# A state-space, attention, expert and feed block on one core: dense products spread evenly beside the attention, gates' rows by transfers, products of zeros in the attention's sums

## The chip, the cores and the metric

One core of a Trainium2 chip runs the whole program in one launch. The metric is the device time of one execution in microseconds (us), lower is better. Engines are called PE (matrix products), PEld (its weight loads), DVE (vector), ACT (activations), POOL, and SP (which only issues transfers here).

## What is computed

2048 tokens of 128 values go through two layers, four residual blocks in all, each on the layer-normed stream. Cut to what matters, with `ln` for a layer norm without weights:

```
x = x + ssd(ln(x))          # Mamba-2 like: projections, conv, 8 heads x 32, state 16, gate, projection
x = x + ffn0(ln(x))         # h = ln(x); a = h + causal attention (16 heads of 8, 2048 x 2048);
                            # a + sum over 8 experts of gate[e] * (gelu(ln(a) @ fc1[e].T + b) @ fc2[e].T + b2)
                            # gate: softmax over the best 2 of 8 logits, 0 for the others
x = x + scan(ln(x))         # Mamba-1 like: projection, conv, silu, 256 channels x 16 states:
                            # h[t] = exp(-n * delta[t]) * h[t-1] + delta[t] * B[n][t] * u[t]
x = x + feed(ln(x))         # gated product 128 -> 512, two products 512 -> 512 with gelu, 512 -> 128
```

All 8 experts are computed for every token, and the gates weigh their results.

## The kernel before, in words

**Tiling.** The tokens are cut into four chunks (c = 0 to 3) of 512. Activations lie with features on the 128 partitions and the 512 tokens of a chunk along the free dimension, so the common product is 128x128 weights with a moving 128x512 operand in f32. The profile records such an f32 product as two MATMULs ("x2" is one product).

**The attention** is cut into jobs (c, g), four heads to a job. `shift` (L287) finds each query's largest score: per step a pair of heads, L302 into the sums `ps_m`, and DVE's L312 takes the maximum. `weighted` (L327) computes the scores anew, keys on the partitions: per step two L352 (one per head of the pair, 32 rows each) and two L358 (they subtract the maximum, 32 rows), into the one buffer `ps_e`; ACT's exp (L362) reads it into `probs`; and per two steps L339 multiplies the probabilities with values and a column of ones, 9 columns a head, into `ps_o`. `in_step` lets `weighted` of a job and `shift` of the next go in step. There are 320 such steps of `weighted`, 32, 64, 96 and 128 for the four chunks; the key blocks on the diagonal are shorter.

**What stands beside it.** The other blocks are Python generators that yield a weight for the work they have just issued. `with_attention` (L200) takes them one after another, and after each yield of weight w it issues attention steps of weight w * RATE. So the distance between two yields of a block sets how many of its products stand together, and how many steps of the attention follow without one. `ssd(1)` to `ssd(3)` go beside the first jobs. Then comes `second_layers`: experts(0); scan(0) and experts(1) abreast; scan(1) and feed(0) abreast; experts(2); feed(1). RATE (L452) is the attention's weight over that of the work meant to lie beside it. What is left of the attention is then issued alone. After it, with more buffers, scan(2) goes together with experts(3), scan(3) with feed(2), and feed(3) alone; experts(3) needs the whole attention. A scheduler moves instructions within dependencies and priorities (the order of issue), so the order on each engine is near this, not equal to it; each engine runs its own queue in order.

**The experts** (L722). Per expert: two transfers bring fc1 and fc2 into `wide` (three buffers, SP's queue). The gates (tokens on partitions) are turned to rows by products with the identity, in two parts of f32r whose sum is exact (`ge2`, `ghi`, L773, `rows_in`); L719 then spreads the row of expert e over all 128 partitions by a product with a selecting matrix, and DVE copies it into `gb` (L785). Four products L789 with gelu on ACT (L790); yield 3.7; four products L794 into one sum `ps_c`; DVE's L796 adds the bias and multiplies by `gb`; POOL adds it up; yield 3.5.

**The scan** (L807). After projections, a convolution (L825, L827), softplus and `du`, each of the 16 states takes: SP's transfer of B's row, spread over the partitions (`bb`), ACT's exp (`da`, L863), DVE's product (L865) and two scans (L867), and a transfer from POOL's queue that adds `db` to a sum in memory (L876). `w_bd` holds B's rows twice (48 columns).

**The feed** (L896). Gate products L911 and L913; yield 7.0; two layers of 4 x 4 products L927, yielding 7.0 after each 8; then L937.

Of the kernel before, what the change touches and what calls it, by code (L numbers as in the profile page):

```python
# [19 lines left out]
P = 128  # L20
# [52 lines left out]
def two_layers(ctx: ExitStack, tc: tile.TileContext, a: dict, out: bass.AP):  # L73
# [125 lines left out]

    def with_attention(stages, rate):  # L200

        due = 0.0
        for w in stages:
            due += 1.0 if w is None else w * rate
            while due > 0:
                w = next(attending_all, 0.0)
                due = 0.0 if not w else due - w
# [41 lines left out]
    def prepare(c):  # L249
# [35 lines left out]
        yield 1.0  # L285

# [40 lines left out]
    def weighted(c, g):  # L327
# [16 lines left out]
        for kb in range(nk):  # L344
# [3 lines left out]
            for i in range(0, 4, 2):  # L348
# [20 lines left out]
                if i == 0 and waiting:  # L369
                    sum_up(*waiting.pop())  # L370
                yield 1.1
# [80 lines left out]
    RATE = (4 * 11.0 + sum(48.0 * (c + 1) for c in range(NC))) / (2.5 * SSD + 2 * (MOE + SCAN + FEED) + 0.6 * MOE)  # L452
# [239 lines left out]
    w_bd = load(wp, "w_bd", [P, 2, 3 * DS], "(k p) o -> p k o", p=P)  # L692
    w_u = load(wp, "w_u", [P, 2, DI], "(k p) o -> p k o", p=P)
    w_dt1 = load(wp, "w_dt1", [3 * DS, DI])
# [7 lines left out]

    zeros = side.line("zeros")
    nc.gpsimd.memset(zeros, 0.0)
    two_rows, minus_low, rows_in = {}, {}, {}
    scratch_b = [tc.dram_tile([DS, C], F32, name=f"scratch_b{i}") for i in range(2)]
    for n in (NE,):
        two_rows[n] = wp.tile([P, n], F32R, name=f"two_rows{n}")
        nc.vector.tensor_tensor(two_rows[n], ident[:, 0:n], ident[:, n : 2 * n], ALU.add)
        minus_low[n] = wp.tile([2 * n, 2 * n], F32R, name=f"minus_low{n}")  # L710
        nc.vector.tensor_scalar(minus_low[n], ident[0 : 2 * n, 0 : 2 * n], 0.0, None, ALU.mult)
        nc.vector.tensor_scalar(minus_low[n][:, n:], ident[0 : 2 * n, n : 2 * n], -1.0, None, ALU.mult)
        rows_in[n] = [wp.tile([P, C], F32R, name=f"rows_in{n}_{i}") for i in range(1)]
        for t in rows_in[n]:
            nc.vector.tensor_copy(t, zeros)

    def spread_row(pg, n, rows_of, i):

        nc.tensor.matmul(pg, two_rows[n][:, i : i + 1].to_broadcast([P, P]), rows_of, start=True, stop=True)  # L719


    def experts(c, z):  # L722
# [34 lines left out]
        ge2 = sp.tile([P, NB, 2, NE], F32, tag="ge2", name="ge2")  # L757
        for i in range(2):
            nc.vector.tensor_tensor(ge2[:, :, i], ge, top.unsqueeze(2).to_broadcast([P, NB, NE]), ALU.mult)
        pgt = z.bank([2 * NE, C])  # L760
        for b in range(NB):
            nc.tensor.matmul(
                pgt[:, b * P : (b + 1) * P],
# [315 lines left out]
```

## Time and profile before

| | |
|---|---|
| median of 7 runs | 1755.42 us (1746.52 to 1764.16) |
| the profiled execution | 1763.77 us; its span, first to last instruction, 1762.1 us |
| mean granted clock of PE | 0.822 |
| moved by transfers | 83.24 MB |

The stages, from windows of the trace (busy us of each engine; clock is the share of PE's full clock that was granted):

| us from the start | what runs | PE | DVE | ACT | clock |
|---|---|---|---|---|---|
| 0 to 151 | ssd(0), part of ssd(1) | 125.5 | 78.0 | 31.4 | 0.88 |
| 151 to 438 | ssd(1) to ssd(3), attention | 270.6 | 169.5 | 82.5 | 0.82 |
| 438 to 1440 | second layer, attention | 883.4 | 533.6 | 476.5 | 0.82 |
| 1440 to 1589 | scan(2), experts(3) | 102.4 | 104.2 | 74.9 | 0.82 |
| 1589 to 1762 | scan(3), feed(2), feed(3) | 110.9 | 88.6 | 60.5 | 0.77 |

How to read it: busy time of PE is counted from start to modelled end, so it grows when the clock is low. A row of a windows view holds from:to, its length, then for each engine busy us and, in brackets, the number of instructions, then the clock, the transfers' share of 16 engines, and GB/s. With a line or tile chosen, only those instructions are counted. The trace starts the attention's steps at 151 and ends them at 1440.

### The profile page before, as it was taken

What the parts mean: (1) busy time and instruction counts of PE and PEld (TensorE: products, weight loads), DVE (VectorE), ACT (ScalarE), POOL (GpSimd) and SP (SyncE); (2) the same over time, 40 slices, a digit from 0 to 9 for tenths busy, and PEclk for the clock granted to TensorE, in tenths of its full rate; (3) what the DMA queues carried; (4) which work ended last, traced back from release to release, by engine and by line L of the source; (5) the groups of instructions that cost most, each with busy time, mean ns of one, the idle gap of its engine ahead of it and who ended that gap; (6) DMA issues with size and microseconds to landing.
All of it is one profiled execution on the core that took longest, in us unless ns stands there. A gap on an engine that the chain in (4) does not pass through costs nothing. (4 is left out here: it accounts for less than half of the span.)

```text
span 1762.1 us, 16427 instructions
## 1 busy us (share of the span) xinstructions
PE 1492.9 (85%) x6306; PEld 648.6 (37%) x6306; DVE 974.0 (55%) x1556; ACT 725.8 (41%) x847; POOL 284.0 (16%) x316
## 2 busy tenths in 40 slices
PE   6898999999899988889987898788998888657628
PEld 3554445444333433233333332333333243223224
DVE  4555546556444574666567677585343026764950
ACT  2212222323444434545344454355653536543522
POOL 4321111211000010111111012020000001440220
PEclk9887888878798978879578977669996899768759
DMA  2000000000100100323220034330000122760850
GB/s 85 1 1 0 1 0 1 1 0 26 40 27 28 30 1 31 77 55 72 60 68 17 31 78 82 86 66 25 24 30 25 36 66 73 163 141 31 184 97 30
DMA packets 62494, 83.24 MB, mean 47 GB/s; under 512 B 4576, under 2 KB 28816, under 8 KB 62416
## 3 DMA queue, kind: packets, MB, share of 16 engines
q0 software_dynamic: 16320, 31.46, 10.3%
q1 hardware_dynamic: 45664, 49.68, 9.1%
q10 hardware_dynamic: 432, 1.06, 0.2%
q8 instruction: 49, 0.80, 0.2%
q14 instruction: 29, 0.24, 0.0%
HBM read 49.55 MB, written 1.18 MB: 29 GB/s over the span
## 5 line engine op out<-in xcount | busy, mean ns | idle before, releaser
L312 DVE TENSOR_REDUCE top<-ps_m 128x2 f32<-128x1024 f32 (+3 forms) x320 | 339.7, 1061 | 288.5 <-PE ps_m L302 166.5
L362 ACT ACTIVATE probs<-ps_e 128x1024 f32<-128x1024 f32 (+3 forms) x320 | 286.3, 895 | 513.3 <-PE ps_e L358 309.6
L302 PE MATMUL ps_m<-kR,qR 32*128 32x512 f32 (+3 forms) x640 | 191.3, 527 | 68.1 <-DVE top L312 57.0
L352 PE MATMUL ps_e<-qR,kR 32*128 32x512 f32 (+3 forms) x640 | 177.2, 525 | 27.9 <-ACT probs L362 27.3
L339 PE MATMUL ps_o<-probs,vv 128*9 128x512 f32 (+3 forms) x1152 | 172.2, 611 | 1.0 <-ACT probs L362 0.9
L302 PEld LDWEIGHTS ps_m<-kR,qR 32*128 32x128 f32 x640 | 79.5, 209 | 246.4 <-DVE top L312 138.1
L867 DVE TENSOR_TENSOR_SCAN db<-da,hlast,db 128x512 f32<-128x512 f32 x128 | 163.0, 1310 | 5.5 <-ACT da L863 3.5
L358 PE MATMUL ps_e<-sh,onesR 32*128 32x512 f32 (+3 forms) x640 | 149.7, 434 | 0.1
L352 PEld LDWEIGHTS ps_e<-qR,kR 32*128 32x128 f32 x640 | 70.4, 207 | 182.0 <-ACT probs L362 106.6
L789 PE MATMUL ps_a<-nT,wide 128*128 128x512 f32 x192 | 116.3, 714 | 6.5 <-ACT h L790 4.3
L794 PE MATMUL ps_c<-h,wide 128*128 128x512 f32 x192 | 103.9, 645 | 0.0
L798 POOL TENSOR_TENSOR acc<-acc,ye 128x512 f32<-128x512 f32 x28 | 43.6, 1557 | 329.2 <-DVE ye L796 329.2
L871 POOL COPY hlast<-db 128x2 f32<-128x2 f32 x48 | 29.3, 611 | 388.7 <-DVE db L867 388.7
L863 ACT ACTIVATE da<-dl 128x1024 f32<-128x1024 f32 x64 | 66.4, 1054 | 51.0 <-DMA db<-db 25.4
L865 DVE TENSOR_TENSOR db<-du,bb 128x1024 f32<-128x1024 f32 x64 | 78.0, 1228 | 15.9 <-issue 11.0
L790 ACT ACTIVATE h<-ps_a,cols 128x512 f32<-128x512 f32 x96 | 63.8, 686 | 55.8 <-PE ps_a L789 55.5
L358 PEld LDWEIGHTS ps_e<-sh,onesR 32*128 32x128 f32 x640 | 77.9, 221 | 3.0 <-issue 1.8
L927 PE MATMUL ps_a<-g,wide 128*128 128x512 f32 x96 | 59.2, 748 | 13.8 <-ACT g L930 13.8
L789 PEld LDWEIGHTS ps_a<-nT,wide 128*128 128x128 f32 x192 | 37.9, 220 | 47.1 <-issue 20.7
L362 ACT ACT_TABLE_LOAD x41 | 52.6, 1283 | 1.3 <-PE ps_e L358 0.6
L927 PE MATMUL ps_a<-h,wide 128*128 128x512 f32 x96 | 50.8, 662 | 1.0 <-ACT g L930 1.0
L375 DVE COPY os<-ps_o 128x512 f32<-128x512 f32 x16 | 10.9, 683 | 70.9 <-PE ps_o L339 70.8
(375 smaller groups left out, 2156.2 us busy)
## 6 DMA issues: line engine op xcount, KB each, us to landing
wide<-in_fc SPq DMA_DIRECT2D x64, 256.0 KB, 3.2
bb<-scratch_b SPq DMA_DIRECT2D x64, 256.0 KB, 3.4
db<-db POOLq DMA_DIRECT2D x32, 512.0 KB, 5.8
u<-db POOLq DMA_DIRECT2D x28, 512.0 KB, 5.8
wide<-in_h SPq DMA_DIRECT2D x16, 512.0 KB, 3.6
wide<-in_w SPq DMA_DIRECT2D x8, 256.0 KB, 2.9
x<-in_x SPq DMA_DIRECT2D x4, 256.0 KB, 5.4
w<-in_w SPq DMA_DIRECT2D x4, 256.0 KB, 3.9
```

What stands on the lines that cost most here:

```text
L302: nc.tensor.matmul(pss[:, j, 0:n], qR[hr, w - P : w], kR[hr, g, kc * C : kc * C + n], start=True, stop=not diag,)
L312: nc.vector.tensor_reduce(top[:, i : i + 2, kc], pss[:, :, 0:n], AX.X, ALU.max)
L339: pv = nc.tensor.matmul(o, v, prs[i // 2][:, i % 2, q0:], start=kb == 0, stop=kb == nk - 1)
L352: nc.tensor.matmul(pss[:, j, q0:], kR[hr, g, kb * P : (kb + 1) * P], qR[hr, q0:], start=True, stop=False)
L358: nc.tensor.matmul(pss[:, j, q0:], onesR[hr], sh[hr, q0:], start=False, stop=not diag)
L362: last = nc.scalar.activation(pr[:, :, q0:], pss[:, :, q0:], AF.Exp, scale=float(1.0 / np.sqrt(np.float32(HD))))
L789: nc.tensor.matmul(ph, we[:, 0, f * P : (f + 1) * P], nT, start=True, stop=True)
L794: nc.tensor.matmul(py, we[:, 1, f * P : (f + 1) * P], hs[f // 2][:, f % 2, :], start=f == 0, stop=f == NF - 1)
L863: in_turn("exp", nc.scalar.activation(da, dl, AF.Exp, scale=-float(n + 1)))
L865: nc.vector.tensor_tensor(db, du, bb.unsqueeze(1).to_broadcast(two), ALU.mult)
L867: nc.vector.tensor_tensor_scan(db[:, j, :], da[:, j, :], db[:, j, :], hlast[:, j, n : n + 1], ALU.mult, ALU.add)
L927: nc.tensor.matmul(ph, w[k // 2][:, k % 2, f * P : (f + 1) * P], h[k // 2][:, k % 2, :], start=k == 0, stop=k == NF - 1)
```

## The change

- **Spreading.** `experts` yields 0.9 after each of the first three products into `ps_c` and 0.8 after the fourth; `feed` yields 3.5 after each two of its gate products, and 0.9 or 0.8 after each single product of L927 (after's L916). `abreast` gets a share for each thread, by which its weights are passed on: 0.3 for a scan, 1.0 for experts and feed. RATE's divisor is 2.5 SSD + 3 MOE + 0.6 SCAN + 2 FEED in place of 2.5 SSD + 2 (MOE + SCAN + FEED) + 0.6 MOE, 401.1 in place of 440.7.
- **Gates by transfers.** The gates' rows are transposed in f32, copied to `gT`, written to memory (after's L762), and a transfer per expert brings row e to all partitions (after's L771). The products and copies with `rows_in`, `minus_low` and `two_rows` go.
- **Zeros.** `full` counts the weight of dense work issued, at most 1.0, less 0.7 per step of the attention. Where it is below 0, a step adds a product of the identity with 128x256 zeros to half of `ps_o` (after's L381), which changes no value, and counts 0.43 for it.
- `w_bd` and `w_dt1` lose the doubled 16 columns and rows.

```diff
+    full = [0.0]
     def with_attention(stages, rate):
         due = 0.0
         for w in stages:
+            full[0] = min(full[0] + (w or 0.0), 1.0)
             due += 1.0 if w is None else w * rate
...
+    zeros = ap.tile([P, 2 * P], F32, name="zeros")
+    nc.gpsimd.memset(zeros, 0.0)
...
                 if i == 0 and waiting:
                     sum_up(*waiting.pop())
+                full[0] -= 0.7
+                if full[0] < 0 and 0 < kb < nk - 1:
+                    nc.tensor.matmul(
+                        po[:, C - 256 :], ident, zeros[:, 0:256], start=False, stop=False, skip_group_check=True
+                    )
+                    full[0] += 256 * 4 / 2400
                 yield 1.1
...
-    RATE = (4 * 11.0 + sum(48.0 * (c + 1) for c in range(NC))) / (2.5 * SSD + 2 * (MOE + SCAN + FEED) + 0.6 * MOE)
+    RATE = (4 * 11.0 + sum(48.0 * (c + 1) for c in range(NC))) / (2.5 * SSD + 3 * MOE + 0.6 * SCAN + 2.0 * FEED)
...
-        pgt = z.bank([2 * NE, C])
...
-        gT = rows_in[NE][0]
-        ghi = z.line("ghi", (2 * NE, C), F32R)
-        nc.vector.tensor_copy(ghi, pgt)
-        nc.tensor.matmul(pgt, minus_low[NE], ghi, start=False, stop=True, skip_group_check=True)
-        nc.vector.tensor_copy(gT[0 : 2 * NE], pgt)
+        pgt = z.bank([NE, C])
+        for b in range(NB):
+            nc.tensor.transpose(pgt[:, b * P : (b + 1) * P], ge[:, b], ident)
+        gT = z.line("gT", (NE, C))
+        nc.vector.tensor_copy(gT, pgt)
+        gates = scratch_g[c % 2]
+        nc.sync.dma_start(gates, gT)
...
-            pg = z.bank([P, C])
-            spread_row(pg, NE, gT, e)
             gb = z.line("gb")
-            nc.vector.tensor_copy(gb, pg)
+            nc.sync.dma_start(gb, gates[e].partition_broadcast(P))
...
                 nc.tensor.matmul(py, we[:, 1, f * P : (f + 1) * P], hs[f // 2][:, f % 2, :], start=f == 0, stop=f == NF - 1)
+                if f < NF - 1:
+                    yield 0.9
...
-            yield 3.5
+            yield 0.8
...
-        yield 7.0
+            if f % 2:
+                yield 3.5
...
                         ph, w[k // 2][:, k % 2, f * P : (f + 1) * P], h[k // 2][:, k % 2, :], start=k == 0, stop=k == NF - 1
                     )
+                    if k < NF - 1:
+                        yield 0.9
                 in_turn("gelu", nc.scalar.activation(g[f // 2][:, f % 2, :], ph, AF.Gelu, scale=col(scale, f)))
-                if f % 2:
-                    yield 7.0
+                yield 0.8
...
                 if w is not None:
-                    t[2] += w
-                    yield w
+                    t[3] += w
+                    yield w * t[2]
...
-        yield from abreast((scan(0, scans), SCAN), (experts(1, side), MOE))
-        yield from abreast((scan(1, scans), SCAN), (feed(0, side), FEED))
+        yield from abreast((scan(0, scans), SCAN, 0.3), (experts(1, side), MOE, 1.0))
+        yield from abreast((scan(1, scans), SCAN, 0.3), (feed(0, side), FEED, 1.0))
```

## The prediction

> **What bounds the kernel now.** I read the engines' shares first, then the 40 slices, then the stages as windows, then single products.
>
> ```profile
> PE 1492.9 (85%) x6306; PEld 648.6 (37%) x6306; DVE 974.0 (55%) x1556; ACT 725.8 (41%) x847; POOL 284.0 (16%) x316
> PE   6898999999899988889987898788998888657628
> PEclk9887888878798978879578977669996899768759
> ```
>
> PE is the engine nearest to its limit, and in four fifths of the slices its busy digit is 8 or 9. But its granted clock (third line) is a 6, 7 or 8 in most slices, and twice a 5. A busy PE at 0.5 does half as much. So the question for this kernel is not only how much PE has to do, but at what clock. The stages between the start of the second layer and the end of the attention, in windows (PE, PEld, DVE, ACT, POOL busy, then the clock):
>
> ```profile
> 438.00:590.00 152.00, 142.98 (x610) 57.52 (x608) 70.46 (x107) 69.82 (x83) 7.61 (x6) 0.90 0.11 34
> 590.00:930.00 340.00, 294.43 (x1208) 111.86 (x1204) 205.39 (x291) 158.34 (x176) 44.35 (x49) 0.78 0.22 51
> 1064.00:1183.00 119.00, 94.79 (x442) 39.53 (x444) 80.91 (x94) 53.21 (x57) 21.33 (x23) 0.66 0.39 78
> 1183.00:1332.00 149.00, 142.13 (x709) 52.46 (x705) 71.06 (x88) 85.63 (x96) 8.93 (x8) 0.97 0.08 25
> 1332.00:1440.00 108.00, 96.35 (x383) 34.11 (x384) 12.29 (x31) 48.96 (x52) 3.79 (x4) 0.79 0.07 22
> ```
>
> They are experts(0); scan(0) with experts(1); the end of scan(1) with feed(0); experts(2); feed(1). Now the instructions of L352 alone, two for each step of the attention (one pair of heads, one key block), and then those that read `wide`, the expert and feed weights (two records to a product):
>
> ```profile
> 1064.00:1183.00 119.00, 23.14 (x66) 9.17 (x66) 0.66 0.39 78
> 1183.00:1332.00 149.00, 23.21 (x98) 9.07 (x96) 0.97 0.08 25
> ```
>
> ```profile
> 1064.00:1183.00 119.00, 11.71 (x18) 3.55 (x18) 0.66 0.39 78
> 1183.00:1332.00 149.00, 65.68 (x126) 21.16 (x126) 0.97 0.08 25
> ```
>
> This is the main reading. The first stage did 33 steps with 9 dense products in 119 us, 3.6 us a step; the second did 49 steps with 63 products in 149 us, 3.04 us a step. Nearly five times the dense work per step, and each step was shorter, because the clock was 0.97 instead of 0.66. (Scan(1), on DVE, is a second difference of the two; I come back to it.) That PE's busy share doesn't decide the clock is seen in two windows of 40 us:
>
> ```profile
> 840.00:880.00 40.00, 38.15 (x99) 13.76 (x100) 18.07 (x23) 15.50 (x18) 5.42 (x6) 0.53 0.27 53
> 1280.00:1320.00 40.00, 38.99 (x183) 13.65 (x181) 16.89 (x18) 23.28 (x25) 2.56 (x2) 1.00 0.08 27
> ```
>
> Both are busy over 95%, one at half the clock, one at full. The first holds 11 records on `wide`, the second 38. The attention's own products fill little of the array: L352, L358 and L302 have 32 rows of 128, and L339 mostly 9 columns of 128. What keeps the clock up seems to be products that use all rows and columns, arriving without long gaps. Here is an attention step at full clock with nothing dense beside it:
>
> ```profile
> 1380.77 1.03 ACT probs L362
> 1382.68 1.03 ACT probs L362
> 1384.59 1.02 ACT probs L362
> ```
>
> From exp to exp it is 1.91 us, of which ACT's exp takes 1.02 and L352 with L358 the rest; that is the floor of a step. One dense product of 128x512 (two records) takes 0.86 us more at full clock: in the chain of waits L927 x2 takes 1.06 us and x4 1.91.
>
> **The change, part by part.**
>
> *Spreading.* I counted, in the order of PE's instructions in both programs, the dense work after each of the 320 steps (f32 columns times four, f32r times two, in units of one 128x512 f32 product). Before, 51 steps stand in runs of three or more with less than half a product after each; after, 4. From step 64 to the end (the second layer's part) the real dense work goes from 358 to 377 units, since feed(1) now ends inside the attention and scan(2)'s first products (after's L808 to L871) stand before the last step. Half of feed(1)'s L927 did so already.
>
> *Zeros.* After's L381 stands 96 times in PE's order: 22 in the first 64 steps, 74 later. The trace of before has no 128x256 f32 product with these operands. The nearest row, 0.86 us for 512 columns, gives 0.43 at full clock and 0.86 at half; nothing, if it falls where PE waits for the exp. So 0 to 82 us; I take 0.43, 41 us in all, since most stand in front of the next L352 on PE's queue, and the step behind waits for them. Whether zeros as data hold the clock up no row can show: the gain of this part lies between none and the whole gain of even work. I take it that they count like other products, the rows of before telling instructions by shape and not by value.
>
> *The attention's part, summed.* After has 414 units in 256 steps (zeros counted as half a unit), 1.62 a step. The stage 1183 to 1332 is the template: by the program's order it had 1.34 units a step, took 3.04 us, at clock 0.97. The 0.28 units more cost 0.24 us, so 3.28 us a step, 840 us. To this I add two things. Scan(0) and scan(1) stand beside 113 of the steps, by the weights: RATE is now 524/401.1 = 1.31, a step of both parts weighs 1.5, so (62 + 0.3 x 46) x 1.31/1.5 = 66 and (40 + 13.8) x 1.31/1.5 = 47; DVE's work for one is 16 states of 1.23 + 2 x 1.31 = 3.85 us, 62 us, and L312's reductions share DVE in order with them. I charge a third of the 124 us, 41 us (0 to 124). ACT's order holds 160 table loads where it held 130, 28 of the 30 inside the attention, as exp and gelu now alternate oftener: 28 x 1.28 = 36 us of ACT, part of it beside PE's work; I charge 24. Sum 905 us, against 1002 now (438 to 1440): **-97 us**.
>
> *First layer's part* (151 to 438, 287 us at 0.82): 22 zeros cost 9 us, and its work isn't cut finer. I take the clock to give the 9 back: 0.
>
> *The gates.* Removed: 32 L719 and 32 L785 on the two rows below, plus L773. Added: four writes of 16 KB and 32 broadcasts of 256 KB on SP's queue. The nearest rows land in 1.6 us (`scratch_b`) and 3.4 us (`bb`).
>
> ```profile
> L785 DVE COPY gb<-ps_a x24: 664/680/692, 458.9 to 1323.0; 128x512 f32<-128x512 f32 x24
> L719 PE MATMUL ps_a<-rows_in,two_rows x24: 401/493/799, 458.1 to 1321.9; 128*128 128x512 f32 x24
> ```
>
> In SP's order the broadcast for expert e stands behind the weights that wait for expert e-2's buffer, so it goes out about one expert early; an expert takes 152/8 = 19 us in the first window, which covers 3.4. Of the copies' 22 us on DVE and L719's 20 us on PE I count nothing in the attention: the template stage had them, so what they cost there stays in the sum as a reserve of a few us. In the tail they were: PE sat idle 19.2 us before L789 for gb's copy. Against that eight broadcasts more, 2.1 MB, at the 160 to 200 GB/s moved there, take 10 to 13 us of queues on which the scans' accumulating transfers already end the chain. I let the two cancel.
>
> *The tail.* DVE was idle for 68 us before the attention's last copy, and scan(2)'s preparation came only then:
>
> ```profile
> 1436.72 0.69 DVE L375 COPY os<-ps_o 128x512 f32<-128x512 f32 x1 [68.30 <-PE ps_o L339]
> ...
> 1485.84 1.21 DVE L865 TENSOR_TENSOR db<-du,bb 128x1024 f32<-128x1024 f32 x1
> ```
>
> From the attention's end to the first state it takes 49 us. In after's order on DVE everything from layer norm to `du` and `u` (L802 to L843) stands ahead of that copy. What is late next is experts(3): its layer norm, gating and first expert, ahead of the first state on DVE; before, its first L796 came at 1474.7, 38 us after the copy, with PE shared. I take 31 us in its place: **-18 us** (-30 to 0). Bd's 16 columns fewer cost and give nothing, as 512 columns are streamed either way.
>
> **Sum.** 1763.8 (this execution's own time, 1762.1 of span) - 97 - 18 = 1649. The median of the runs shown is 1755.4, 8 us lower, so **1640**.
>
> A rule of the Trainium skill speaks against this: "TensorE: Matmul & The Clock Gate", section "What's actually happening", says that the monitor sets the clock by how busy PE has recently been, and throttles it after an idle window of about 3.4 us. By that, the window 840 to 880, 95% busy, would have had a full clock, and it had 0.53. Under the rule taken literally zeros and spreading would give no clock, and the sum would be the slower rival below. The trace decides against it here: it is the filling of the array that goes with the clock.
>
> **Rivals.**
>
> *No clock gained, zeros paid (slower).* If the clock follows something else, or products of zeros don't count and the even work isn't enough, the step keeps its present cost and the added work is paid. Before's own steps (from start to start of L352), sorted by the units that stand in three successive ones, took for the three 8.6 us (none), 8.5 (two), 10.7 (four), 12.9 (six); weighted with after's counts, they give 1022 us in place of 986 for the same 253 steps, +36; with the first layer's 9 and the tail's -18, 1791 here, **1782** by the median. It decides if the stages with 1.6 units a step show a clock under 0.85.
>
> *DVE and ACT become the bound.* In 590 to 930 DVE is busy 205 of 340 us, in order, with L312 and the scans; after gives these stages a quarter fewer steps (66 for 86, by RATE 1.19 without shares). If their steps don't shrink below 3.6 us, and the table loads (36 us) fall wholly on the path, the gain in the attention is 10 to 40 us: with the tail's 18 **1712**, by the median. For it speak the 57 us in which PE waits for DVE's L312; against it that no engine but PE is busy over 70% in any of these windows.
>
> *The scheduler undoes the spreading.* PE's order excludes it: 4 steps in long runs, not 51.
>
> *More than forecast.* With the template's step kept at 3.04 us, 778 us, the attention gains 224 and the whole ends near **1515** by the median.
>
> **Chances.** Forecast (1570 to 1700) 0.70; DVE and ACT (1700 to 1750) 0.14; no clock (1755 to 1800) 0.10; more than forecast (under 1570) 0.06. The range 1570 to 1740 leaves out 0.06 below and about 0.13 above. Faster by over 0.5% (9 us, about what a measurement of this kernel can tell from no change): 0.70 + 0.06 + 0.12 = 0.88; within it 0.03; slower 0.09.
>
> **What would show it.** Right: clock digits of 9 from the second layer on; the 256 steps (512 records) of L352's successor L360 in the second layer's part at 3.2 to 3.6 us each; the attention's last copy near 1340; first L853 within 31 us of it. Wrong: the same clock with 96 more products of L381; or a full clock with PE idle, behind ACT's table loads and L320's reductions. The first would overthrow the whole argument, the second only its size.

## The result and the profile after

The changed kernel took **1765.62 us** (median of 27 executions, 1746.75 to 1773.77), the kernel before 1752.55 on the same chips (67 executions): ratio **1.0083**, 95% interval 1.0066 to 1.0099. It is slower by 0.8%, clear of the noise, where the forecast was 1640 us. The profiled execution of after has a span of 1763.9 us and lies at its kernel's median; that of before (1763.8 us, clock 0.822) is one of its kernel's longer ones, so its stages are shown some us longer, and its clock lower, than is usual for it.

From the page of after: PE's line of the busy times, then PE's busy tenths and the granted clock in 40 slices.

```profile
PE 1497.6 (85%) x6446; PEld 656.1 (37%) x6446; DVE 953.4 (54%) x1512; ACT 765.5 (43%) x877; POOL 274.6 (16%) x316
...
PE   5898999999999898978988888999999887557638
...
PEclk9897796898989896986979867899999897768769
```

PE is as busy as before. The clock's row has five 9s in turn from the 27th slice on (1147 us and later), but from the 17th to the 26th (706 to 1147 us) it still goes between 6 and 9. So the clock is up in one place and not in another, and the stages show which. Windows of after (PE, PEld, DVE, ACT, POOL busy, clock): experts(0) and what leads to it; scan(0), scan(1) with experts(1) and feed(0); experts(2); feed(1).

```profile
428.00:686.00 258.00, 235.76 (x1029) 99.30 (x1028) 125.22 (x241) 102.51 (x120) 22.84 (x27) 0.85 0.12 34
686.00:1131.00 445.00, 382.63 (x1590) 147.56 (x1589) 299.62 (x375) 236.24 (x252) 72.48 (x83) 0.82 0.34 76
1131.00:1300.00 169.00, 157.53 (x768) 59.89 (x766) 71.06 (x89) 88.63 (x99) 10.18 (x9) 0.96 0.13 40
1300.00:1451.00 151.00, 135.33 (x647) 50.52 (x644) 44.29 (x65) 92.21 (x94) 3.81 (x4) 0.93 0.09 27
```

The same windows of after for L360 alone (two instructions to a step of the attention; PE, PEld, clock), for the scans' stage and that of experts(2):

```profile
686.00:1131.00 445.00, 56.20 (x200) 21.41 (x200) 0.82 0.34 76
1131.00:1300.00 169.00, 24.36 (x100) 9.53 (x100) 0.96 0.13 40
```

and for the dense products, those that read `wide` (two records to a product):

```profile
686.00:1131.00 445.00, 124.68 (x208) 39.83 (x206) 0.82 0.34 76
1131.00:1300.00 169.00, 67.15 (x128) 21.67 (x128) 0.96 0.13 40
```

In the scans' stage 100 steps and 104 dense products took 445 us, 4.45 us a step at clock 0.82; in experts(2)'s, 50 steps and 64 products took 169 us, 3.38 us a step at 0.96. The dense work per step is nearly alike now (1.04 and 1.28) and evenly spread in both. The first is not faster for it: before, the stage 590 to 1183 (290 instructions of L352, 145 steps, in 593 us) took 4.1 us a step. The two paces are not quite like with like: a step of this stage now has 0.4 units more beside it (1.6 for 1.2, 0.35 us at full clock), and 100 steps share the two scans where 145 did; the runs below are the firmer ground. The forecast's 3.28 us nearly held in the stage that it was read from, and not in the one that it was carried to. Nor did it hold in experts(0), which has no scan beside it either: from 479 to 648 us 41 steps and 64 products took 169 us, 4.1 us a step at clock 0.91. Steps 64 to 320 as a whole took 997 us before (438 to 1435) and 1023 after (428 to 1451), 74 products of zeros among them.

What one step of the scans' stage looks like is in the timeline of after (start, duration, engine, instruction, and in brackets the idle time before it and what ended it):

```profile
990.38 1.27 DVE L855 TENSOR_TENSOR_SCAN db<-da,hlast,db 128x512 f32<-128x512 f32 x1
...
991.63 1.27 DVE L855 TENSOR_TENSOR_SCAN db<-da,hlast,db 128x512 f32<-128x512 f32 x1
991.96 1.28 ACT L921 ACT_TABLE_LOAD   x1
...
992.21 0.28 PE L366 MATMUL ps_e<-sh,onesR 32*128 32x256 f32 x2
992.83 1.20 DVE L320 TENSOR_REDUCE top<-ps_m 128x2 f32<-128x1024 f32 x1
...
993.25 0.69 ACT L921 ACTIVATE g<-ps_a,cols 128x512 f32<-128x512 f32 x1
...
994.08 0.51 PE L310 MATMUL ps_m<-kR,qR 32*128 32x512 f32 x2 [1.59 <-DVE top L320]
...
994.71 2.02 PE L916 MATMUL ps_a<-h,wide 128*128 128x512 f32 x2
995.00 1.28 ACT L370 ACT_TABLE_LOAD   x1 [1.06 <-PE ps_e L368]
```

L310 needs `ps_m`, which L320 must have read; L320 stands on DVE behind the scan's two L855. So PE is idle for 1.59 us, and the dense product L916 that the change had put there can't use the gap: it stands behind L310 in PE's queue. On ACT a gelu (L921) brings two table loads, 1.28 us before it and 1.28 us before the next exp. And the L916 that follows runs at half the clock: 2.02 us for two records, where the one before this stretch, at 988.69, took 1.08.

### The profile page after: what moved, and what is told of

Read it like the earlier page. It is cut to its first block, busy times and chain, and to the rows that moved or that the text cites. A ratio compares the mean times of both kernels' runs of the same rounds, so it can differ in the third digit from the quotient of the medians.

```text
span 1763.9 us, 16756 instructions
## 1 busy us (share of the span) xinstructions
PE 1497.6 (85%) x6446; PEld 656.1 (37%) x6446; DVE 953.4 (54%) x1512; ACT 765.5 (43%) x877; POOL 274.6 (16%) x316
## 3 DMA queue, kind: packets, MB, share of 16 engines
HBM read 57.90 MB, written 1.25 MB: 34 GB/s over the span
## 4 chain that ended last, share of the span: by engine, by line
PE 60%; DVE 17%; ACT 8%; issue 7%; DMA 4%; POOL 3%; SPq 0%; POOLq 0%; ACTq 0%; DVEq 0%
PE ps_o L347 7%; PE ps_m L310 5%; PE ps_a L775 5%; PE ps_e L360 5%; DVE db L855 5%; PE ps_c L780 4%; DVE top L320 4%; PE ps_a L916 3%; PE ps_e L366 3%; PE ps_o L381 3%; ACT probs L370 3%; DMA db<-db 2%; DVE db L853 2%; PE ps_c L605 2%; PE ps_a L580 2%
## 5 line engine op out<-in xcount | busy, mean ns | idle before, releaser
L320 DVE TENSOR_REDUCE top<-ps_m 128x2 f32<-128x1024 f32 (+3 forms) x320 | 339.6, 1061 | 331.9 <-PE ps_m L310 187.8
L310 PE MATMUL ps_m<-kR,qR 32*128 32x512 f32 (+3 forms) x640 | 174.1, 508 | 50.9 <-DVE top L320 41.6
L360 PE MATMUL ps_e<-qR,kR 32*128 32x512 f32 (+3 forms) x640 | 165.4, 498 | 26.0 <-ACT probs L370 24.4
L855 DVE TENSOR_TENSOR_SCAN db<-da,hlast,db 128x512 f32<-128x512 f32 x128 | 165.1, 1331 | 15.1 <-ACT da L851 13.1
L347 PE MATMUL ps_o<-probs,vv 128*9 128x512 f32 (+3 forms) x1152 | 161.9, 568 | 1.5 <-ACT probs L370 1.5
L310 PEld LDWEIGHTS ps_m<-kR,qR 32*128 32x128 f32 x640 | 71.5, 202 | 195.6 <-DVE top L320 100.0
L366 PE MATMUL ps_e<-sh,onesR 32*128 32x512 f32 (+3 forms) x640 | 142.4, 414 | 0.8 <-DVE sh L332 0.8
L360 PEld LDWEIGHTS ps_e<-qR,kR 32*128 32x128 f32 x640 | 65.3, 195 | 172.2 <-ACT probs L370 94.6
L775 PE MATMUL ps_a<-nT,wide 128*128 128x512 f32 x192 | 110.5, 687 | 5.5 <-ACT h L776 5.4
L853 DVE TENSOR_TENSOR db<-du,bb 128x1024 f32<-128x1024 f32 x64 | 79.3, 1245 | 17.0 <-DMA db<-db 9.2
L916 PE MATMUL ps_a<-g,wide 128*128 128x512 f32 x96 | 66.4, 823 | 16.7 <-ACT g L921 13.5
L859 POOL COPY hlast<-db 128x2 f32<-128x2 f32 x48 | 20.5, 428 | 379.3 <-DVE db L855 373.8
L366 PEld LDWEIGHTS ps_e<-sh,onesR 32*128 32x128 f32 x640 | 71.8, 205 | 6.6 <-issue 5.4
L381 PE MATMUL ps_o<-zeros,ident 128*128 128x256 f32 x192 | 69.0, 443 | 0.0
L916 PE MATMUL ps_a<-h,wide 128*128 128x512 f32 x96 | 51.3, 660 | 6.1 <-ACT g L921 6.1
```

The costliest lines, as they stand in the source:

```text
L310: nc.tensor.matmul(pss[:, j, 0:n], qR[hr, w - P : w], kR[hr, g, kc * C : kc * C + n], start=True, stop=not diag,)
L320: nc.vector.tensor_reduce(top[:, i : i + 2, kc], pss[:, :, 0:n], AX.X, ALU.max)
L347: pv = nc.tensor.matmul(o, v, prs[i // 2][:, i % 2, q0:], start=kb == 0, stop=kb == nk - 1)
L360: nc.tensor.matmul(pss[:, j, q0:], kR[hr, g, kb * P : (kb + 1) * P], qR[hr, q0:], start=True, stop=False)
L366: nc.tensor.matmul(pss[:, j, q0:], onesR[hr], sh[hr, q0:], start=False, stop=not diag)
L381: nc.tensor.matmul(po[:, C - 256 :], ident, zeros[:, 0:256], start=False, stop=False, skip_group_check=True)
```

## The experiments

Each was timed beside the kernel before on the same chip, and the ratio is to that. Some runs leave instructions out or put another function in the place of gelu, so their results are not the block's; they are there for their times. "Gates alone" and such names are used below. Times are medians; the clock is the median over a kernel's executions; lines are those of after where nothing else is said.

### First: the three parts one by one

After the result three readings stood against one another, A, B and C of the expectations: the zeros cost more than they give back; the zeros carry the clock; the broadcasts crowd the tail.

**The change without its zeros**

```diff
-                full[0] -= 0.7
-                if full[0] < 0 and 0 < kb < nk - 1:
-                    nc.tensor.matmul(po[:, C - 256 :], ident, zeros[:, 0:256], ...)
-                    full[0] += 256 * 4 / 2400
```

> The changed kernel without the 96 products of zeros (results unchanged). Theory A, the zeros cost more than the clock they give: 96 x 0.43 = 41 us of PE go, the mean clock falls from 0.851 only a little (0.83 or more), and the time falls by 15 to 40 us, to 1725-1750, below before's 1752. Theory B, the zeros carry the clock and something else in the change costs: clock back to 0.82, time 1770 to 1800. In between (1755 to 1770): the zeros pay just for themselves.

1740.2 us, ratio 0.9932 (0.9904 to 0.9959). The zeros cost 25 us.

**The kernel before with zeros** (the counter `full` and L381 put in; the trace has 148 of the products, 296 records)

> The kernel before with the zeros alone, set by the same counter; as its dense work is less even, the counter puts 147 of them. Theory A: 147 x 0.43 = 63 us of PE are added, the clock rises to 0.86 or more, and the time is 0 to 40 us over before's, 1752 to 1792. Theory B: the clock's gain outweighs them, 1700 to 1745.

1769.6 us, 1.008 (1.0044 to 1.0115): +17 us (14 by the ratio) for 63 us of products (148 x 0.43), clock 0.860 for 0.829.

**The kernel before with the spreading alone** (RATE, shares, yields; 158 table loads for 130)

> The kernel before with the spreading alone (yields, shares, RATE), without zeros and with the gates as before. Theory A (steps outside experts(2) are held by DVE and ACT, not by the clock, and 28 more table loads and more work inside the attention are paid): 1755 to 1785. Theory B, my prediction's reading (even work raises the clock and so shortens steps): 1690 to 1735 at a clock of 0.86 or more.

1758.4 us, 1.0056 (1.0022 to 1.009): +6 us, where the forecast had its whole gain. The clock did rise (0.840 for 0.829), but span times clock rose too (from 1452 to 1477 us), by work or waits that are added; what the clock won went there.

**The kernel before with the gates alone** (transfers for L719 and L785, 16 columns fewer)

> The kernel before with the gates' rows by transfers alone (and the 16 columns fewer). Theory C, the 32 broadcasts crowd the transfers of the scans in the tail: slower than before by 5 to 20 us, 1757 to 1772, the tail after the attention longer than 327 us. Otherwise the removed copies and products show: 5 to 20 us faster, 1732 to 1747. The clock stays at 0.82.

1731.5 us, 0.9876 (0.9836 to 0.9917): **-21 us**, the only part that gains. The clock is 0.839 for 0.829, where it was expected to stay. Added to before, gates -21, then spreading (1740.2 - 1731.5) +9 and zeros +25 give +13, which is the change. On the gates alone the spreading gave no clock either (0.840 for 0.839).

### Second: why the spreading gave nothing

The expectations set two theories against one another. Filling theory, the forecast's: the clock follows how much of the array the products fill, so even products raise it. Stall theory: PE waits behind DVE's scans and ACT's tables, the clock falls in those waits, and products behind a blocked queue can't help.

**Without the scans** of the first two chunks (left out: 64 L867 of the kernel before)

```diff
-            for j in range(2):
+            for j in range(2 if c > 1 else 0):
                 nc.vector.tensor_tensor_scan(
```

> The kernel before, leaving out both scans L867 of each state for scan(0) and scan(1) (32 states, 64 instructions of 1.31 us, 84 us of DVE beside the attention); L865, the transfers and all products stay. Stall theory (the clock falls in windows in which PE waits for DVE's maxima or ACT's exps, because those engines are busy with other work, and not where the order has few dense products): the clock in the stages with the scans (0.77) rises to 0.85 or more with no product added, and the time falls by 50 to 110 us. Filling theory (my prediction's: the number of dense products per step sets the clock): the clock there stays near 0.77 and the time falls by under 40 us.

1699.0 us, 0.9699 (0.9631 to 0.9768), -53 us. The stage of the scans in windows of before, and of this run:

```profile
652.00:1195.00 543.00, 461.67 (x1995) 178.08 (x1993) 347.34 (x434) 254.17 (x277) 77.89 (x85) 0.78 0.26 59
```

```profile
644.00:1119.00 475.00, 423.90 (x1957) 166.59 (x1956) 271.23 (x366) 250.43 (x273) 75.65 (x85) 0.83 0.31 67
```

76 us less of DVE, and the stage is 68 us shorter at a clock of 0.83 for 0.78, with no product added (it also holds 132 steps for 136, some 15 us). DVE is busy 64% there, and yet of the 80 us of scans that are left out 53 are off the whole run. The stall theory's clock of 0.85 wasn't reached.

**The change with tanh for gelu** (the first three chunks of experts and first two of the feed; the feed's line is shown, that of the experts has `c > 2`)

```diff
-    in_turn("gelu", nc.scalar.activation(g[f // 2][:, f % 2, :], ph, AF.Gelu, ...))
+    in_turn("gelu", nc.scalar.activation(g[f // 2][:, f % 2, :], ph, AF.Gelu if c > 1 else AF.Tanh, ...))
```

> The changed kernel with tanh in place of gelu for the experts and feeds beside the attention (experts 0 to 2, feed 0 and 1), a function that needs no other table than exp: 74 table loads are left of 160, 110 us of ACT go; all else is the same. Stall theory: the exps come earlier, PE waits less, the time falls by 25 to 70 us and the clock rises by 0.01 or more. Filling theory: ACT was busy 43% and the loads lie beside PE's work; within 10 us of the changed kernel's 1765.

1691.6 us, 0.9664 (0.9607 to 0.9721): 74 us below the change. The gelus' own time stays (0.69 us each); what goes are 86 table loads. The group that names it, the loads ahead of the attention's exp, of after and then of this run:

```profile
L370 ACT ACT_TABLE_LOAD x52 | 66.7, 1283 | 4.3 <-PE ps_e L366 2.4 <-PE ps_e L368 1.1
```

```profile
L370 ACT ACT_TABLE_LOAD x12 | 15.4, 1283 | 0.3
```

86 x 1.28 = 110 us of ACT, an engine that is busy 43%, were worth 74 us, a little over the 25 to 70 expected.

**Spreading without the feed's yields** (on the kernel before; 134 loads)

> The kernel before with RATE, the shares and the experts' finer yields, but the feed's yields as before: 134 table loads, where the whole spreading had 158 and before has 130. If the feed's 24 more table loads are what spreading costs, the time is 5 to 25 us under that of the whole spreading (1758), 1733 to 1753. If not, it stays at 1755 to 1760.

1745.1 us, 0.9982 (0.995 to 1.0014). 13 us less than the whole spreading, which has 24 loads more: the feed's single products, each with a gelu between the attention's exps, cost more than they give.

**Zeros in every step that takes them** (on the kernel before; the trace has 256 of the products, 512 records)

```diff
+                if 0 < kb < nk - 1:
+                    nc.tensor.matmul(po[:, C - 256 :], ident, zeros[:, 0:256], ...)
```

> The kernel before with a product of zeros in every step in which one may stand: 252 of them, 108 us of PE at full clock. Stall theory: zeros cannot be issued while PE stalls, so the clock still falls about as often; they pay back about half their price (0.03 of clock per 63 us were seen), and the time rises by 20 to 60 us, to 1772-1812, at a clock of 0.87 to 0.90. Filling theory: every step is now over the threshold, the clock goes to 0.94 or more, and the time is at or under 1752.

1790.0 us, 1.0215 (1.0142 to 1.0287), clock 0.875. Zeros do raise the clock (0.832 for before), and pay back some 72 of their 109 us (256 products).

### Third: cheaper ways, on the gates alone

**Gates, pace, shares and experts' yields**

> The gates by transfers, the new pace and the threads' shares, and the experts' yields within the second product; the feed's yields as before and no zeros. If the parts add up, this is the run with the gates alone (1731.5 us) less what the spreading without the feed's yields gave on the kernel before (1745.1 against 1752.5, 7 us): 1724 us, 1716 to 1732, ratio near 0.984. Filling theory (even products raise the clock): the clock over the run rises by 0.02 or more against the gates alone and the time falls by 20 us or more, below 1712. Stall theory: the clock moves by less than 0.01, and what the table loads cost sets the rest.

1731.2 us, 0.9873 (0.9839 to 0.9907): nothing beyond the gates.

**Gates, and yields between the scan instructions**

```diff
             for j in range(2):
+                yield 0.6
                 nc.vector.tensor_tensor_scan(
...
-            yield 2.0
+            yield 0.8
```

> The gates by transfers, and beside them one edit in the scans: of the yield of 2.0 units behind each state, 0.6 is put ahead of each of its two scan instructions, so that the attention's maxima on VectorE can come between them and not only behind a whole state (about 3.9 us of VectorE); the sum of the yields is the same, and 8 table loads more come of it (138 for 130). Stall theory: TensorE waits less often behind VectorE, so the stage of the scans gets 10 to 25 us shorter, less 4 to 7 us for the loads: 1712 to 1728 us, clock up by 0.005 to 0.015. Filling theory: no product is added or spread, so the time stays at 1731 or rises by the loads, 1731 to 1740 us.

1730.8 us, 0.9858 (0.983 to 0.9886). The stall theory's 10 to 25 us didn't come. So it is not that two scans stand together; letting maxima between them moves the wait and doesn't remove it: in the profiles PE waits 56.8 us for the maxima (L310 for L320) with the gates alone, and 59.6 here.

**Gates, and the feed's products by four**

```diff
-                if f % 2:
-                    yield 7.0
+                if f == NF - 1:
+                    yield 14.0
```

> The gates by transfers, and beside them one edit in the feed: its yield comes behind four groups of products, not behind two, so that four gelus follow one another: 119 table loads for 130, and its sixteen products stand in one block of 14 us of TensorE. Stall theory with the price per load of the earlier runs (0.5 to 0.9 us): 6 to 10 us less than the gates alone, 1721 to 1726 us. Filling theory: the products are bunched more, the attention's steps between are emptier, so the clock falls and the time rises by 5 to 15 us, 1736 to 1747 us.

1758.4 us, 1.0011 (0.9988 to 1.0035): 27 us slower than the gates alone (24 by the ratios), with 11 loads fewer. Here the filling theory had the sign right, though its 5 to 15 us were too little, and the stall theory was wrong.

**The three together**

> The three together: gates, pace and shares and experts' yields, scan yields, feed by fours (124 table loads). Stall theory, by the sum of its terms: 7 us from the experts' spreading, 5 to 15 us from the scans, 6 to 10 us from the feed, so 1700 to 1715 us. Filling theory: the scans' edit gives nothing and the feed's costs, 1725 to 1740 us.

1738.7 us, 0.9905 (0.9871 to 0.9939). The time lies in the filling theory's range (1725 to 1740), and for its reason: by the single runs the scans' edit gives nothing, and it is the fours that cost. But beside the new shares they cost 7 us and not 27.

### Fourth: both theories apart, with the loads taken out

Fours cost 27 us, singles 13 (against pairs). The loads run the other way from the bunching, so they were taken out: tanh for gelu in all four kernels.

**Gates alone with tanh** (pairs, 65 loads)

> The gates by transfers, with tanh for gelu in the first three experts' and the first two feeds' chunks (so the function is another; its duration is the same, and it shares a table with the attention's exponentials): 65 table loads for 130. By the price of the earlier run (74 us for 86 loads): 56 us less than the gates alone, 1675 us, 1660 to 1690. It is the base of the two that follow.

1698.4 us, 0.9673 (0.9646 to 0.97). That is 33 us less than the gates alone (36 by the ratios), where 56 were expected: a load is worth less here than in the change.

**The change without zeros, with tanh** (singles, 74 loads)

> The change without its zeros, with tanh for gelu as in e13: spread singly, 74 loads. Loads theory (spreading fills the array, and the table loads that it adds took the gain back): with the loads out it is 30 us or more below e13, 1645 us or less, clock up by 0.02 or more. Stall theory (spreading gives next to nothing, since TensorE's queue stands behind VectorE): within 15 us of e13, 1660 to 1685 us. Against the run of the change with tanh (1691.6), zeros out: 20 to 30 us less, 1662 to 1672, if the zeros' price does not hang on the loads.

1665.6 us, 0.9483 (0.9454 to 0.9512): 33 us below the pairs, as the loads theory had it, with 0.016 more of clock (it had 0.02). The change with zeros and tanh took 1691.6, so the zeros cost 26 us here too: their price doesn't hang on the loads.

**Gates and fours with tanh** (62 loads)

> e13 with the feed's products by four (62 loads): if bunching itself cost the 27 us of the run by fours, it is 25 to 40 us above e13, 1700 to 1715 us; if it was another cause that hangs on gelu's tables, it is within 8 us of e13.

1731.1 us, 0.9855 (0.9824 to 0.9887): 33 us above the pairs, so bunching itself costs.

So with the loads out, the order that the forecast argued from is there: fours 1731, pairs 1698, singles 1666, 33 us for each step. Span times clock, which is PE's time at full clock, is 1424, 1423 and 1421 us, and the clock 0.824, 0.839 and 0.854: **the whole difference is clock.** From the first product of experts(0) to the attention's end, in windows of fours, pairs and singles:

```profile
443.00:1395.00 952.00, 836.47 (x3714) 319.27 (x3710) 504.73 (x676) 386.95 (x458) 106.53 (x110) 0.82 0.21 52
```

```profile
451.00:1367.00 916.00, 811.69 (x3697) 307.72 (x3697) 502.56 (x676) 384.86 (x457) 105.70 (x110) 0.85 0.22 53
```

```profile
467.00:1352.00 885.00, 783.29 (x3705) 299.49 (x3703) 508.82 (x687) 393.44 (x462) 101.23 (x111) 0.88 0.24 58
```

DVE's and ACT's busy times are alike within 3%; the clock differs (0.82, 0.85, 0.88), and PE's busy time with it. From fours to pairs only the feed's yields differ. From pairs to singles the pace and shares do too, and by the profiles 15 us lie ahead of the attention's end (1367, 1352) and 11 behind it, where scan(2)'s preparation is already done (the two executions profiled differ by 26 us, the medians by 33). So the gain is real, but a fraction of the forecast's, and with gelu's own tables the same edit costs 9 us.

**Singles with tanh and without the scans** (the 64 scan instructions left out as above)

> e14 without the scan instructions of the first two chunks (64 of them, 82 us of VectorE, left out; tanh for gelu as there). Stall theory: what holds the clock down are waits behind VectorE and ScalarE, so with both out it rises: 45 to 60 us less than e14 (53 us was the price on the kernel before), 1605 to 1625 us, the clock of the second part at 0.92 or above. If the forecast's figure holds at all (0.97 beside the attention), 1580 us or less. Filling theory alone: no product is added, so the time falls by VectorE's own share at most, and the clock stays within 0.01 of e14.

1611.3 us, 0.9172 (0.9144 to 0.92), 54 us less than with the scans.

```profile
463.00:1296.00 833.00, 754.73 (x3703) 290.99 (x3702) 434.94 (x623) 392.29 (x462) 97.69 (x111) 0.92 0.25 61
```

L360 has 496 instructions in this window, 248 steps, so a step takes 3.36 us at clock 0.92. Only here, with neither wait, the whole stretch goes at about the pace that the forecast gave it, 3.28 us (and that had zeros in it); the clock of 0.97 that it was to have isn't reached even so.

### Fifth: can the change keep its gelu?

**Singles, the gelus held back in pairs** (137 loads, no zeros, nothing left out)

```diff
-                in_turn("gelu", nc.scalar.activation(g[f // 2][:, f % 2, :], ph, AF.Gelu, ...))
+                held_ph.append((f, ph))
+                if f % 2:
+                    for i, p in held_ph:
+                        in_turn("gelu", nc.scalar.activation(g[i // 2][:, i % 2, :], p, AF.Gelu, ...))
+                    held_ph = []
```

> The change without its zeros, the feed's products spread singly as in the change, but its gelus held back and issued two together (the first of a pair waits in its PSUM bank for the second): 137 table loads for 160, nothing left out. Loads theory: 23 loads fewer at 0.5 to 0.9 us are 12 to 20 us off the 1740 of the run without zeros, so 1718 to 1730 us, and the clock rises by 0.005 to 0.01. If the loads are not what took the gain back: 1735 to 1745 us.

1733.7 us, 0.989 (0.9853 to 0.9928). 6 us under the change without zeros, by intervals that overlap, for 23 loads fewer (12 to 20 us were expected); no faster than the gates alone. Inconclusive: the held products also keep both buffers of `ps_a`, which the scan beside them needs, and no run takes that apart.

**The same, with the scans' products on POOL**

```diff
-            nc.vector.tensor_tensor(db, du, bb..., ALU.mult)
+            (nc.gpsimd if c < 2 else nc.vector).tensor_tensor(db, du, bb..., ALU.mult)
```

> e17, with the product ahead of each scan in the first two chunks on GpSimd for VectorE: 32 products of 128x1024, 40 us of VectorE. Stall theory: the price of VectorE's time in the runs without scans, 54 us for 82, gives 26 us less than e17, 15 to 30. Against it: GpSimd took 1.5 us for a product of half the size, so about 3 us stand in each state's own chain in place of 1.25; if that chain becomes the bound, or GpSimd slows VectorE, the time is that of e17 or up to 20 us above.

1740.3 us, 0.9937 (0.9906 to 0.9968). 40 us less work on DVE, and 7 us slower. The groups of the scan instructions (there L849; idle time before them and what ended it last) without and with the products on POOL:

```profile
L849 DVE TENSOR_TENSOR_SCAN db<-da,hlast,db 128x512 f32<-128x512 f32 x128 | 164.0, 1320 | 19.0 <-ACT da L845 17.3
```

```profile
L849 DVE TENSOR_TENSOR_SCAN db<-da,hlast,db 128x512 f32<-128x512 f32 x128 | 169.0, 1358 | 42.9 <-ACT da L845 21.1 <-POOL db L847 20.3
L847 POOL TENSOR_TENSOR db<-du,bb 128x1024 f32<-128x1024 f32 x32 | 78.1, 2444 | 90.9 <-DVE du L835 75.8 <-issue 15.1
```

POOL takes 2.44 us for what DVE does in 1.25, and DVE now stands idle 24 us more ahead of the scans, with the attention's maxima queued behind: PE waits 57.2 us for them (L310 for L320), where it was 48.3 in the run without POOL's products. The wait was moved, not removed.

## Why the prediction was wrong

| term | forecast, us | measured, us | by |
|---|---|---|---|
| spreading, beside the attention | -97, zeros' 32 in it: -129 | +9 | without zeros against gates alone |
| zeros | +32 there, +9 - 9 in the first layer | +25 | after against without zeros |
| gates | 0 | -21 | gates alone |
| tail | -18 | within the above; profiled -14 | last copy of `os` to the end, 325.4 and 311.0 |
| sum | -115 | +13 | |

**The step that failed** is the one called the main reading, with the sum built on it: that the stage 1183 to 1332 is "the template" for all 256 steps because its clock of 0.97 came from its even dense products, while scan(1) was only "a second difference of the two", charged with a third of DVE's time. The stage that was carried over has no scan beside it. In after it took 3.38 us a step, and the scans' stage, given the same evenness, 4.45. The runs price the waits that the template lacked, or that the spreading adds. The 64 scan instructions, 82 us of DVE, cost 54 us, where 41 were charged for all 124 us of the two scans (53 on the kernel before, so the price does not hang on the order). The loads cost far above the 24 that were charged: spreading (with the tail that goes with it) gives 33 us where loads are few (65 and 74) and takes 9 where they are not (130 and 160), so the loads took **42 us** back, all that it gave and more. Taking loads out gave 0.51 us for each with the gates alone (33 us for 65) and 0.87 with singles (75 us for 86). How much of the 42 is their number and how much their place, no run tells. The number added isn't all of it: with the gelus held back in pairs the spreading has 7 loads more than the gates alone and still gives nothing (1733.7 for 1731.5), unless the buffers that it holds are what costs.

Taken in a row, the runs come down from before's 1752 us to 1611: 21 us by the gates, 33 by leaving out 65 loads, 33 by the spreading, 54 by leaving out the scans. So what the forecast took for the price of uneven products (129 us) was in the main the price of other waits; evenness is worth 33 us, and that only where gelu's loads are out. What the row does not explain is experts(0) in after: without a scan, and with as many loads (16) as experts(2), it took 4.1 us a step for 1.9 units. By the pace of experts(2) (3.38 us for 1.55 units) and 0.86 us for each further unit it would be 3.7; the rest is open. The template was too low there too.

The mechanism of that step was half right. In the traces of before, of after and of the runs with tanh the clock is either full or half, and its changes lie whole multiples of 3.41 us apart. I cut the second layer's part into windows of 3.41 us on these changes, and worked out for each the filled share of the array (rows x columns x cycles of all products) and PE's busy share. Of two windows at full clock, one followed by a drop and one not, the first is the less filled in 98% of pairs, before and after. But PE's busy share orders them as well (99% and 98%), so the falls don't tell the two apart. What empties a window at full clock is mostly PE standing idle: each one with PE busy under 0.60 (16 before, 17 after) was followed by half the clock, and none with PE busy over 0.90. For the clock's return neither share decides so well (filling orders 89% of the pairs of windows at half before and 70% after, the busy share 89% and 84%). For filling speaks that nine windows in a row, 846 to 876 us of before, stayed at half with PE busy 0.87 to 1.00.

Drops come as often after the change as before (27 and 26). What the change shortens is the time until the clock comes back: 103 windows at half before, 80 after. The three orders with tanh show the same: by fours, by pairs and singly the clock falls 24, 25 and 22 times, and is at half for 99, 78 and 62 windows. Without the scans it falls 16 times for 22, and 40 windows for 62 are at half. So even products help a clock that is low; they don't stop it from falling while PE's queue is blocked. These counts are from one profile each.

The Trainium skill's rule that the prediction weighed and set aside ("TensorE: Matmul & The Clock Gate", section "What's actually happening": the monitor looks at how busy PE was, and throttles after an idle window) was the nearer one for the falls, though a window with PE idle for 40% of it was enough here. For how long the clock stays low it is not enough: windows at half had PE busy 0.86 before and 0.85 after, and the nine above still more.

**Zeros.** The price was right to the microsecond. Over all executions span times clock goes from 1461 without to 1502 with them, 41 us = 96 x 0.43. They count in the clock, which rose from 0.840 to 0.853, and in the other two runs with zeros too; with them counted as full products the 98% above holds in after, without them it is about 95%. But within each of these kernels an execution with 0.01 more of clock is 10 to 14 us shorter, so 0.013 give back some 15 of the 41. The forecast let them give more than they cost.

The instruction's own row in after (two records to a product, which overlap; ns of a record, min/median/max, to its modelled end; busy in all 69.0 us, 0.72 for each of the 96):

```profile
L381 PE MATMUL ps_o<-zeros,ident x192: 379/435/796, 179.2 to 1447.1; 128*128 128x256 f32 x192
```

**Gates.** The step said that the copies and products cost "nothing in the attention", as a reserve in the template. They were 22 us of DVE and some 20 of PE, 24 of the 32 in the attention, and taking them away gave 21 us; which of the two gave it, no run tells. That the broadcasts hide was right (no wait for `gb` is left); they land early enough in after (KB, median us from issue to landing):

```profile
gb<-scratch_g SPq DMA_DIRECT2D x32, 256.0 KB, 3.9
```

**First layer.** Forecast 0; from the attention's start to its 64th step 279 us after (149 to 428) and 287 before (151 to 438), at clock 0.85 and 0.82. These steps have zeros in them, and each profile is a single one, so this stays a reading.

**Tail.** The first L853 was to come within 31 us of the last copy. The timeline of after:

```profile
1452.87 0.69 DVE L389 COPY os<-ps_o 128x512 f32<-128x512 f32 x1 [1.74 <-PE ps_o L347]
...
1482.95 1.22 DVE L853 TENSOR_TENSOR db<-du,bb 128x1024 f32<-128x1024 f32 x1
```

It came 30.1 us behind it, 49.1 before. The tail as a whole gained 14 us of the 18.

**The rivals.** "No clock gained, zeros paid" named the right side, and its condition, a clock under 0.85 where steps have 1.6 units, was met in the scans' stage (0.82 at 1.6 units). Its time, 1782, has no gain from the gates; with their 21 it would be 1761, against 1766. It was given 0.10. "DVE and ACT become the bound" named the right engines, with the right doubt (steps that don't shrink below 3.6 us; table loads on the path), but left the attention a gain of 10 to 40 us where it lost 26, with 32 us of zeros in that.

**Fastest.** The gates alone (1731.5 us, 0.9876), with or without the experts' yields or those in the scans (1731.2 and 1730.8), beat before by 21 us and after by 34; the three can't be told apart. Why the scans of two chunks cost 54 us of their 81 (the 64 L855 in after's second window), while neither finer yields nor POOL lowers that, is open: in both ways that were tried PE waited for the maxima as long as before or longer.

## What to carry to other kernels

A stage that runs well is a template only for stages with the same queues beside it: before carrying its pace over, ask of each engine whose results PE waits for what else stands in that engine's queue, for work placed behind a blocked instruction can't fill the gap it leaves. Multiply span by granted clock for each run: what an edit adds in work and what it wins in clock come apart at once, and filler that raises the clock must win more than it adds (here it won 15 of 41 us, 46 of 63 and 72 of 109). Where activations of two table sets alternate with a chain's own, price the loads too, however idle the engine looks: here they cost 0.51 to 0.87 of their 1.28 us each, and the spreading that added 30 of them lost all that it gives without them.

## What the runs showed of the hardware

- The clock is full or half (in one trace, that of the change without zeros, 0.95 or half), and its changes lie whole multiples of 3.41 us apart. Falls go with a window that is little filled and, as much, with one in which PE is idle: all 33 windows at full clock with PE busy under 0.60 were followed by half (16 before, 17 after, second layer's part), so 40% idle is enough.
- A busy PE isn't enough for the return: nine windows in a row with PE busy 0.87 to 1.00 stayed at half, their filled share 0.20 to 0.45. Over all windows of that part one threshold of 0.40 on the filled share foretells the next window's clock in 88% (before) and 89% (after), the best on PE's busy share in 82% and 87%.
- Products of zeros hold the clock up: 96, 148 and 256 of them gave +0.013, +0.031 and +0.043, for 41, 63 and 109 us of work; none of the three paid for itself.
- With the work unchanged, three ways of bunching it (by four, by two, and singly with other shares) gave clocks of 0.824, 0.839 and 0.854 over the run and times of 1731, 1698 and 1666 us.
- 86 table loads of 1.28 us on an engine that is busy 43% were worth 74 us.
